# Attention layer with 96 units: projections, output products and row sums gathered in every second unit

## The chip, the core and the metric

The kernel runs on one core of a Trainium2 chip. The time is the device time of one launch in microseconds (us), the median of three runs. Beside these runs there is one execution recorded by the hardware profiler. Its engines are called PE (matrix products), PEld (loading of weights for PE), DVE, ACT and POOL (GpSimd) in the views, and SP issues most of the DMAs.

## What is computed

Four layers work on x of shape (4, 256, 48, 48) in float32: four samples of 2304 positions with 256 channels. Each layer adds its result to x, after a group norm of x. Only the first layer is touched by the change:

```python
def _L0_conv_ref(x, w_qkv, w_out, b_out):        # HEADS = 8, DIM_HEAD = 64, SCALE = 10
    qkv = jnp.einsum('oc,bchw->bohw', w_qkv, x)
    q, k, v = jnp.split(qkv, 3, axis=1)
    q, k, v = map(to_heads, (q, k, v))           # (b, 8, 64, 2304)
    q, k = _l2norm_last(q), _l2norm_last(k)      # over the 2304 positions
    sim = jnp.einsum('bhdi,bhdj->bhij', q, k) * SCALE
    attn = jax.nn.softmax(sim, axis=-1)
    out = jnp.einsum('bhij,bhdj->bhid', attn, v)
    ...
    return jnp.einsum('oc,bchw->bohw', w_out, out) + b_out[None, :, None, None]
...
x = x + _L0_conv_ref(_gn(x), L0_conv_w_qkv, L0_conv_w_out, L0_conv_b_out)
```

Layer 1 is a gate made of a pooled and blurred map with 81 distinct taps a channel; layer 2 is an attention with one head; layer 3 a depthwise convolution with a norm.

## The kernel before

**Phases, units, ticks.** Layer 0 has 16 phases, one for each sample `b` and pair of heads `p`. A phase has `NCH` = 6 units, each a slice of `SL` = 384 query positions (`l0_unit`), so there are 96 units. A unit has `NG` = 9 ticks, each for two blocks of 128 key positions. All units of layers 0 and 2 run in one list, in `attend`. The order of the instructions on every engine is written out by hand: the loop of `attend` issues them tick by tick, and engines run that order, waiting only for each other's results and buffers.

In a tick `attend` issues, in this order:

- `scores` for two key blocks: eight products with 64x64 pieces of the array (the profile records each float32 product twice), then two exponentials on ACT into `pt` tiles (eight buffers, so four ticks' worth). The scores go to `sc` tiles, of which there are two, of two banks each.
- `add_up` for the tick before: two DVE additions of `pt` tiles into `acc`, the row sums. In the first sample every second tick (`PAIRED`) adds its two `pt` tiles on POOL first (`half`, L355).
- what is entered for this tick in `due` and in `fills`, the latter in the order of a rank, and the generators of other layers (`lanes`): layer 1 of sample b-1 runs beside layer 0 of sample b.
- `weigh` for the tick before: eight products `av<-pt,v` with 64x64 pieces.
- `take_taps`: some of the tap products of layer 1 (`tap`, L992, on ACT) that wait in `taps_due`, as many as `QUOTA` says for the slot of the tick in its unit; one more is taken behind each job whose rank is in `EVICTED`.

**The stretch of full-array products.** In the third tick of a unit (slot 2, `AT_CHUNK`), three kinds of job are entered in `fills`:

- `chunk(s)`: the projections of one slice of 384 positions for the next phase: `query` and `key` (`qk`, L661, two float32 products of 128x128 by 384 columns each) and `values` (L695, six of 128 columns). They go to `pj` tiles, of which there are two, and ACT moves them out (L681, L700) and squares q and k (L686). `fetch` loads the x slices, two in advance.
- `total`: the sums over partitions of `acc` of the unit that ended two ticks before (L386, eight products with 128x32 pieces, 96 columns); ACT copies them to `row` and a DMA to `l`. Three ticks later `invert` takes reciprocals on DVE and SP's DMAs spread them to `rinv`; four ticks after that `divide` (POOL, L424) multiplies the output, which `fold` (POOL, L420) has formed.
- `out_proj`: 11 ticks after a unit's end, its two output products (`part`, L759) and their additions onto x on DVE (`onto`, L775). From the second sample on `part(0)` uses an `sc` tile, `part(1)` a `pj` tile.

So each unit of layer 0 has one such stretch between its scores and its `weigh`. The matrix products of the group norms (`of_means`, `of_squares`) and `biased` are put into these stretches too. The strips of layer 1 (`strips`) start when the norm's `nb` is there, and reduce a round of taps on DVE (L1015) in slots 2, 4, 6 and 8; a reduction first issues those of its taps that have not been issued yet.

Of the kernel before, what the change touches and what calls it, by code (L numbers as in the profile page):

```python
# [9 lines left out]
F32 = mybir.dt.float32  # L10
# [4 lines left out]
P = 128  # L15
# [63 lines left out]
def usual_path(  # L79
# [109 lines left out]
    of_k, of_out, clock = {}, {}, {"t": -1}  # L189
# [12 lines left out]
    def gn(b, res, halves=range(NK), slices=range(NSL), first=False, placed=False):  # L202
# [62 lines left out]
        if placed:  # L265

            t = clock["t"] + 1
            t += (AT_AFTER - t) % NG
            fills.setdefault(t, []).extend([(3.1, of_means), (3.3, squares)])
            fills.setdefault(t + NG, []).extend([(3.1, of_squares), (3.3, inverse)])  # L270
            due.setdefault(t + NG + 3, []).append(done)
            yield 1
            return
# [34 lines left out]
    op = main.enter_context(tc.tile_pool(name="o", bufs=2))  # L308
    ppool = main.enter_context(tc.tile_pool(name="pt", bufs=8))
    apool = main.enter_context(tc.tile_pool(name="acc", bufs=2))  # L310
    hpool = main.enter_context(tc.tile_pool(name="half", bufs=3))
# [37 lines left out]
    def add_up(u, g):  # L349
# [3 lines left out]
        if g in u["paired"]:  # L353
            half = hpool.tile([P, 2, SL], F32, tag="half", name="half")
            nc.gpsimd.tensor_add(half, pts[0], pts[1])  # L355
            pts = [half]
            ready, u["terms"] = terms, pts
        else:
            ready, u["terms"] = terms + pts, []
# [17 lines left out]
    def total(u):  # L377

        if of_out.get("t") == clock["t"]:
            ps = of_out["ps"][:, 392 : 392 + QC]  # L380
        else:
            ps = pj_tile()[:, :QC]
        for e in range(2):
            for j in range(4):
# [4 lines left out]
                )  # L389
        row = small.tile([P, QC], F32, tag="row", name="row")  # L390
        nc.scalar.copy(row, ps)  # L391
# [3 lines left out]
    def invert(u):  # L395
        ls = small.tile([P, LW], F32, tag="ls", name="ls")
        nc.vector.reciprocal(ls, u["l"])
        u["rinv"] = rpool.tile([P, SL], F32, tag="rinv", name="rinv")
# [29 lines left out]
    def total_here(u):  # L428
# [4 lines left out]
        u["rinv"] = rpool.tile([P, SL], F32, tag="rinv", name="rinv")  # L433
# [5 lines left out]
    def total_final(u):  # L439
# [12 lines left out]
        u["part"] = rpool.tile([P, SL], F32, tag="rinv", name="rinv")[:, :QC]  # L452
# [34 lines left out]
    EVICTED = (1, 2, 3.2, 4.3)  # L487
    AT_TOTAL, AT_FOLD, AT_INVERT, AT_DIVIDE, AT_AFTER = 3, 2, 5, 9, 11
    AT_CHUNK = AT_AFTER % NG

    def last(u, t):
# [17 lines left out]
        else:  # L509
            at_total = AT_TOTAL if "shift" in u["of"] else AT_CHUNK  # L510
            todo = [
                (fills, at_total, (4.1, lambda: total(u))), (due, AT_FOLD, lambda: fold(u, nc.gpsimd)),
                (due, AT_INVERT, lambda: invert(u)),
                (due, AT_DIVIDE, lambda: divide(u, nc.gpsimd)),
            ]
            after = AT_AFTER
# [77 lines left out]
    def project(b, norm, pair):  # L594
# [109 lines left out]
        def chunk(s):  # L704

            def query():
                qk(s, 0)()
# [2452 lines left out]
```

## Time and profile before

| | |
|---|---|
| median of three runs | 3393.66 us (3392.78 to 3393.75) |
| the profiled execution, its own time | 3394.24 us |
| its span from first to last instruction | 3392.5 us |
| PE, DVE, ACT, POOL busy | 3361.0, 2548.5, 2284.9, 618.3 us |
| granted PE clock | 0.999 |
| first tick of layer 0 to the first of layer 2 (timeline) | 39.98 to 2846.24 us |

The span is what the trace covers; the own time has 1.7 us more around it. Of a group of instructions the views give the line, the engine, the operation, the tiles as out<-in, the shape and the count, then the busy time, the mean of one in ns, and the idle time of the engine just before it with what ended it.

### The profile page before, as it was taken

What the parts mean: (1) busy time and instruction counts of PE and PEld (TensorE: products, weight loads), DVE (VectorE), ACT (ScalarE), POOL (GpSimd) and SP (SyncE); (2) the same over time, 40 slices, a digit from 0 to 9 for tenths busy, and PEclk for the clock granted to TensorE, in tenths of its full rate; (3) what the DMA queues carried; (4) which work ended last, traced back from release to release, by engine and by line L of the source; (5) the groups of instructions that cost most, each with busy time, mean ns of one, the idle gap of its engine ahead of it and who ended that gap; (6) DMA issues with size and microseconds to landing.
All of it is one profiled execution on the core that took longest, in us unless ns stands there. A gap on an engine that the chain in (4) does not pass through costs nothing.

```text
span 3392.5 us, 89388 instructions
## 1 busy us (share of the span) xinstructions
PE 3361.0 (99%) x38014; PEld 1692.1 (50%) x38014; DVE 2548.5 (75%) x3425; ACT 2284.9 (67%) x3680; POOL 618.3 (18%) x617
## 2 busy tenths in 40 slices
PE   9999999999999999999999999999999999999997
PEld 5555555555555555555554555555554444454543
DVE  3456545568788888787988787777887888977877
ACT  5565656555786687556876885658867865555576
POOL 3433333331111001011111000111110110221133
PEclk9999999999999999999999999999999999999999
DMA  2211111111111111131111111111111110231067
GB/s 93 50 24 27 23 27 22 26 22 27 19 32 23 27 16 31 15 87 18 27 23 27 23 27 23 25 23 27 23 23 23 24 26 11 46 73 21 7 161 231
DMA packets 113176, 127.38 MB, mean 38 GB/s; under 512 B 43056, under 2 KB 103424, under 8 KB 112256
## 3 DMA queue, kind: packets, MB, share of 16 engines
q1 hardware_dynamic: 111520, 119.67, 17.5%
q8 instruction: 300, 4.92, 0.6%
q10 hardware_dynamic: 1248, 1.91, 0.2%
q14 instruction: 108, 0.88, 0.1%
HBM read 56.99 MB, written 11.80 MB: 20 GB/s over the span
## 4 chain that ended last, share of the span: by engine, by line
PE 94%; DVE 3%; ACT 1%; issue 0%; DMA 0%; POOL 0%; SPq 0%; DVEq 0%; POOLq 0%; ACTq 0%
PE av L344 37%; PE sc L324 36%; PE pj L661 8%; PE pj L695 4%; PE pj L759 3%; PE pj L386 1%; PE sc L759 1%; DVE acc L373 1%; PE cv L1977 1%; PE pj L1249 1%; PE pj L1102 1%; PE pj L1290 0%; PE pj L1324 0%; DVE sh L1839 0%; DVE pad L1795 0%
## 5 line engine op out<-in xcount | busy, mean ns | idle before, releaser
L330 ACT ACTIVATE pt<-sc 128x768 f32<-128x768 f32 x1944 | 1473.4, 810 | 739.4 <-PE sc L324 727.3
L373 DVE TENSOR_TENSOR acc<-acc,pt 128x768 f32<-128x768 f32 x1534 | 1529.1, 997 | 179.8 <-ACT pt L330 77.0
L344 PE MATMUL av<-pt,v 64*64 64x384 f32 x13824 | 1274.8, 484 | 0.0
L324 PE MATMUL sc<-q,k 64*64 64x384 f32 x13824 | 1270.0, 482 | 0.5 <-ACT pt L330 0.5
L324 PEld LDWEIGHTS sc<-q,k 64*64 64x64 f32 x13824 | 525.4, 133 | 589.5 <-issue 555.1
L344 PEld LDWEIGHTS av<-pt,v 64*64 64x64 f32 x13824 | 518.2, 133 | 568.4 <-issue 521.5
L424 POOL TENSOR_TENSOR o<-o,rinv 128x384 f32<-128x384 f32 x95 | 121.9, 1283 | 1694.6 <-DMA rinv<-rinv 1684.5
L992 ACT ACTIVATE prod<-pd,wt 128x256 f32<-128x256 f32 x486 | 340.6, 761 | 0.2
L775 DVE SCALAR_TENSOR_TENSOR x<-pj,bo,x 128x384 f32<-128x384 f32 x122 | 75.4, 618 | 278.3 <-ACT row L391 207.0
L661 PE MATMUL pj<-xs,w 128*128 128x384 f32 (+1 forms) x720 | 268.9, 496 | 0.0
L355 POOL TENSOR_TENSOR half<-pt 128x768 f32<-128x768 f32 x96 | 176.0, 1833 | 377.5 <-ACT pt L330 316.1
L373 DVE TENSOR_TENSOR acc<-acc,half 128x768 f32<-128x768 f32 x96 | 91.8, 956 | 120.4 <-POOL half L355 120.2
L661 PEld LDWEIGHTS pj<-xs,w 128*128 128x128 f32 x720 | 124.5, 190 | 93.6 <-issue 32.9
L1015 DVE TENSOR_REDUCE prod<-prod 128x256 f32<-128x1280 f32 x114 | 168.8, 1480 | 1.0 <-ACT prod L992 1.0
L344 PE MATMUL av<-pt,qv 64*64 64x384 f32 x1728 | 163.8, 487 | 0.0
L324 PE MATMUL sc<-qv,kd 64*64 64x384 f32 x1728 | 161.9, 482 | 0.0
L695 PEld LDWEIGHTS pj<-w,xs 128*128 128x128 f32 x1080 | 134.5, 191 | 24.1 <-issue 1.2
L367 DVE TENSOR_TENSOR acc<-pt 128x768 f32<-128x768 f32 x108 | 126.2, 1169 | 25.8 <-ACT pt L330 25.6
L695 PE MATMUL pj<-w,xs 128*128 128x128 f32 x1080 | 135.0, 275 | 0.0
L420 POOL TENSOR_TENSOR o<-raw 128x384 f32<-128x384 f32 x95 | 120.3, 1267 | 45.2 <-ACT raw L416 44.2
L416 ACT COPY raw<-av 128x768 f32<-128x768 f32 x108 | 86.4, 800 | 51.1 <-PE av L344 50.1
L700 ACT COPY v<-pj 128x384 f32<-128x384 f32 x96 | 46.0, 479 | 92.3 <-PE pj L695 92.3
(318 smaller groups left out, 2293.6 us busy)
## 6 DMA issues: line engine op xcount, KB each, us to landing
xs<-in_x_dram SPq DMA_DIRECT2D x90, 384.0 KB
sh<-pad SPq DMA_DIRECT2D x122, 162.2 KB
rinv<-rinv SPq DMA_DIRECT2D x208, 94.5 KB
out_dram<-x SPq DMA_DIRECT2D x23, 384.0 KB
w<-in_wqkv_dram SPq DMA_DIRECT2D x32, 192.0 KB
x<-in_x_dram SPq DMA_DIRECT2D x4, 1152.0 KB
x<-in_x_dram SPq DMA_DIRECT2D x9, 384.0 KB
rinv<-ls SPq DMA_DIRECT2D x208, 1.5 KB
```

The costliest lines, as they stand in the source:

```text
L324: nc.tensor.matmul(ps[c * D : (c + 1) * D, h, :SL], lhsT=u["of"]["k"][r, j0 : j0 + D], rhs=u["of"]["q"][r, u["qc"]], start=True, stop=True,)
L330: nc.scalar.activation(pt, ps[:, :, :SL], AF.Exp, scale=u["scale"])
L344: nc.tensor.matmul(u["av"][h * D : (h + 1) * D, half, :SL], lhsT=value(u, j, h)[r], rhs=pt[r, h, :], start=j == 0, stop=j == JB - 1,)
L355: nc.gpsimd.tensor_add(half, pts[0], pts[1])
L367: nc.vector.tensor_add(u["acc"], ready[0], ready[1])
L373: nc.vector.tensor_add(u["acc"], u["acc"], term)
L424: eng.tensor_mul(o, o, u["rinv"])
L661: nc.tensor.matmul(ps[:, :n], lhsT=at["w"][:, k, t, :], rhs=xs[s][:, k, :n], start=k == 0, stop=k == NK - 1,)
L695: nc.tensor.matmul(ps[:, i * P : (i + 1) * P], lhsT=xs[s][:, k, i * P : (i + 1) * P], rhs=at["w"][:, k, 2, :], start=k == 0, stop=k == NK - 1,
L759: nc.tensor.matmul(ps[:, :n], lhsT=wo[:, p, k * P : (k + 1) * P], rhs=o["o"][:, :n], start=True, stop=True,)
L992: nc.scalar.activation(bufs[n % 3][:, :, min(n, 1) + i].rearrange("p (r c) -> p r c", c=AS), pd[:, PAD + dr : PAD + dr + AS, PAD + dc : PA ...
L1015: nc.vector.tensor_reduce(to, bufs[n % 3][:, :, : min(n, 1) + len(taps)], AX.X, ALU.add)
```

## The change

Up to tick `ALONE` (810, the start of the last of the 16 phases), the jobs of the stretch are gathered in the odd units. `place_at` moves a tick that falls into an even unit on by one unit; the first unit of samples 1, 2 and 3 is excepted. Two slices are projected in the odd unit, with ranks 1 to 1.5 for the first and 2 to 4.3 for the second. The totals of two units go to one `pj` tile, and their copies on ACT become a job of their own (`read_total`). The two output products of a unit go to the two banks of one `sc` tile, and its two additions onto x follow together (`both`); two units take both `sc` tiles. `invert`, `divide` and the output products of a unit come up to two units later than before, and `o`, `acc` and `rinv` get one more buffer each. The group norms that run `placed` are moved by the same rule. `fold` comes one tick later. `PAIRED` is dropped: all additions into `acc` are DVE's. From tick 810 on the stretches stay as they were.

```diff
@@ -186,7 +186,7 @@
 
 
     GN_TICKS = NSL + 4
-    of_k, of_out, clock = {}, {}, {"t": -1}
+    of_k, of_out, of_sums, clock = {}, {}, {}, {"t": -1}
 
     WARM = 160
 
@@ -266,9 +266,11 @@
 
             t = clock["t"] + 1
             t += (AT_AFTER - t) % NG
+            t = t if placed == "soon" else place_at(t)
             fills.setdefault(t, []).extend([(3.1, of_means), (3.3, squares)])
-            fills.setdefault(t + NG, []).extend([(3.1, of_squares), (3.3, inverse)])
-            due.setdefault(t + NG + 3, []).append(done)
+            t = place_at(t + NG)
+            fills.setdefault(t, []).extend([(3.1, of_squares), (3.3, inverse)])
+            due.setdefault(t + 3, []).append(done)
             yield 1
             return
         yield 3
@@ -305,10 +307,9 @@
     xsp = keep.enter_context(tc.tile_pool(name="xs", bufs=2))
     big = main.enter_context(tc.tile_pool(name="big", bufs=2))
     wqp = main.enter_context(tc.tile_pool(name="wq", bufs=2))
-    op = main.enter_context(tc.tile_pool(name="o", bufs=2))
+    op = main.enter_context(tc.tile_pool(name="o", bufs=3))
     ppool = main.enter_context(tc.tile_pool(name="pt", bufs=8))
-    apool = main.enter_context(tc.tile_pool(name="acc", bufs=2))
-    hpool = main.enter_context(tc.tile_pool(name="half", bufs=3))
+    apool = main.enter_context(tc.tile_pool(name="acc", bufs=3))
     rpool = main.enter_context(tc.tile_pool(name="rinv", bufs=1))
     lp = main.enter_context(tc.tile_pool(name="l1", bufs=1))
 
@@ -350,13 +351,7 @@
 
         pts = [u["pt"][j] for j in range(g * G, (g + 1) * G)]
         terms = u.setdefault("terms", [])
-        if g in u["paired"]:
-            half = hpool.tile([P, 2, SL], F32, tag="half", name="half")
-            nc.gpsimd.tensor_add(half, pts[0], pts[1])
-            pts = [half]
-            ready, u["terms"] = terms, pts
-        else:
-            ready, u["terms"] = terms + pts, []
+        ready, u["terms"] = terms + pts, []
         if g == NG - 1:
             ready, u["terms"] = ready + u["terms"], []
             if u.get("final"):
@@ -378,8 +373,12 @@
 
         if of_out.get("t") == clock["t"]:
             ps = of_out["ps"][:, 392 : 392 + QC]
+        elif of_sums.get("t") == clock["t"]:
+            ps = of_sums["ps"][:, 128 : 128 + QC]
         else:
-            ps = pj_tile()[:, :QC]
+            of_sums["ps"], of_sums["t"] = pj_tile(), clock["t"]
+            ps = of_sums["ps"][:, :QC]
+        u["sums"] = ps
         for e in range(2):
             for j in range(4):
                 h, q = j // 2, 2 * (j % 2) + e
@@ -387,15 +386,17 @@
                     ps[32 * j : 32 * j + 32], lhsT=step1[:, 16 - 16 * e : 48 - 16 * e],
                     rhs=u["acc"][:, h, q * QC : (q + 1) * QC], start=e == 0, stop=e == 1,
                 )
+
+    def read_total(u):
         row = small.tile([P, QC], F32, tag="row", name="row")
-        nc.scalar.copy(row, ps)
+        nc.scalar.copy(row, u["sums"])
         u["l"] = small.tile([P, LW], F32, tag="l", name="l")
         nc.sync.dma_start(u["l"], row[0 : P : 16, :].rearrange("g (p w) -> g p w", w=LW))
 
     def invert(u):
         ls = small.tile([P, LW], F32, tag="ls", name="ls")
         nc.vector.reciprocal(ls, u["l"])
-        u["rinv"] = rpool.tile([P, SL], F32, tag="rinv", name="rinv")
+        u["rinv"] = rpool.tile([P, SL], F32, tag="rinv", name="rinv", bufs=2)
         for c in HALVES:
             r0 = c.start
             nc.sync.dma_start(
@@ -430,7 +431,7 @@
         ps = pj_tile()
         for h, c in enumerate(HALVES):
             nc.tensor.matmul(ps[c, :SL], lhsT=ones, rhs=u["acc"][:, h, :], start=True, stop=True)
-        u["rinv"] = rpool.tile([P, SL], F32, tag="rinv", name="rinv")
+        u["rinv"] = rpool.tile([P, SL], F32, tag="rinv", name="rinv", bufs=2)
         nc.vector.reciprocal(u["rinv"], ps[:, :SL])
         u["l"] = ps[:, :SL]
         if "shift" not in u["of"]:
@@ -449,7 +450,7 @@
                         rhs=term[:, h, q * QC : (q + 1) * QC], start=i == 0 and e == 0,
                         stop=i == len(terms) - 1 and e == 1,
                     )
-        u["part"] = rpool.tile([P, SL], F32, tag="rinv", name="rinv")[:, :QC]
+        u["part"] = rpool.tile([P, SL], F32, tag="rinv", name="rinv", bufs=2)[:, :QC]
         nc.vector.reciprocal(u["part"], ps)
         u["l"] = ps
 
@@ -484,9 +485,17 @@
         del taps_due[:n]
 
     FREE = 10**6
-    EVICTED = (1, 2, 3.2, 4.3)
+    EVICTED = (1, 1.2, 1.45, 1.5, 2, 2.2, 3.2, 4.3)
     AT_TOTAL, AT_FOLD, AT_INVERT, AT_DIVIDE, AT_AFTER = 3, 2, 5, 9, 11
     AT_CHUNK = AT_AFTER % NG
+    PHASE = NCH * NG
+    ALONE = (B * NPAIR - 1) * PHASE
+
+    def place_at(t):
+
+        while t < ALONE and (t // NG) % 2 == 0 and (t % (NPAIR * PHASE) >= NG or t < NG):
+            t += NG
+        return t
 
     def last(u, t):
 
@@ -507,14 +516,20 @@
                     todo.append((due, 2, lambda: note(u)))
             after = 3
         else:
-            at_total = AT_TOTAL if "shift" in u["of"] else AT_CHUNK
+            two = "shift" in u["of"]
+            at_total = AT_TOTAL if two else place_at(t + AT_CHUNK) - t
+            late = 0 if two else at_total - AT_CHUNK
             todo = [
-                (fills, at_total, (4.1, lambda: total(u))), (due, AT_FOLD, lambda: fold(u, nc.gpsimd)),
-                (due, AT_INVERT, lambda: invert(u)),
-                (due, AT_DIVIDE, lambda: divide(u, nc.gpsimd)),
+                (fills, at_total, (4.1, lambda: total(u))),
+                (fills, at_total, (4.15, lambda: read_total(u))),
+                (due, AT_FOLD + (not two), lambda: fold(u, nc.gpsimd)),
+                (due, AT_INVERT + late, lambda: invert(u)),
+                (due, AT_DIVIDE + late, lambda: divide(u, nc.gpsimd)),
             ]
-            after = AT_AFTER
-        todo += [(fills, after, fn) for fn in u["after"]]
+            after = AT_AFTER + late
+            if not two:
+                after = place_at(t + after) - t
+        todo += [(fills, after, fn) for fn in u["after"](t + after)]
         for when, dt, fn in todo:
             when.setdefault(t + dt, []).append(fn)
 
@@ -703,6 +718,8 @@
 
         def chunk(s):
 
+            early = s % 2 == 0
+
             def query():
                 qk(s, 0)()
 
@@ -715,8 +732,9 @@
                     fetch(s + 2)
 
             return [
-                (1, query), (2, lambda: values(s)), (2.2, lambda: square(s, 0)), (3, key),
-                (3.2, lambda: at["evict"]()), (4.3, end),
+                (1 if early else 2, query), (1.2 if early else 2.2, lambda: values(s)),
+                (1.25 if early else 2.25, lambda: square(s, 0)), (1.4 if early else 3, key),
+                (1.45 if early else 3.2, lambda: at["evict"]()), (1.5 if early else 4.3, end),
             ]
 
         def scale():
@@ -745,15 +763,22 @@
             ],
         }
 
+    outs = {}
+
     def out_proj(b, p, c, pair, o):
 
         cols = slice(c * SL, (c + 1) * SL)
 
         of = {}
+        alone = False
 
         def part(k):
-            of[k] = ps = pj_tile() if k or b == 0 or soon else sc_tile()[:, 0, :]
-            if k:
+            if alone:
+                of[k] = ps = pj_tile() if k or soon else sc_tile()[:, 0, :]
+            else:
+                of["two"] = of["two"] if k else sc_tile()
+                of[k] = ps = of["two"][:, k, :]
+            if k and alone:
                 of_out["ps"], of_out["t"] = ps, clock["t"]
             n = SL + (c == 0)
             nc.tensor.matmul(
@@ -780,13 +805,27 @@
             part(0)
             onto(0)
 
+        def both():
+            onto(0)
+            onto(1)
+
         end = b == B - 1 and p == NPAIR - 1
         soon = end and c >= NCH - 2
-        return [
-            (0.5 if soon else 1.5 if b else 0, first),
-            *[(0.6 if end and c == NCH - 1 else r, fn)
-              for r, fn in ((4, lambda: part(1)), (4.2, lambda: onto(1)))],
-        ]
+
+        def jobs(t):
+            nonlocal alone
+            alone = t >= ALONE
+            if alone:
+                return [
+                    (0.5 if soon else 1.5, first),
+                    *[(0.6 if end and c == NCH - 1 else r, fn)
+                      for r, fn in ((4, lambda: part(1)), (4.2, lambda: onto(1)))],
+                ]
+            n = outs.get(t, 0)
+            outs[t] = n + 1
+            return [(n + 1.1, lambda: part(0)), (n + 1.3, lambda: part(1)), (n + 1.35, both)]
+
+        return jobs
 
     def l0_unit(b, p, c, pair):
         hold = {}
@@ -799,7 +838,7 @@
             return hold["o"][:, :SL]
 
         return {
-            "pt": {}, "qc": slice(c * SL, (c + 1) * SL), "paired": () if b else PAIRED,
+            "pt": {}, "qc": slice(c * SL, (c + 1) * SL),
             "soon": b == B - 1 and p == NPAIR - 1 and c == NCH - 1,
             "scale": 1.0, "of": pair, "o": o_tile,
             "after": out_proj(b, p, c, pair, hold),
@@ -1360,8 +1399,8 @@
 
     def l2_unit(b, c, s2):
         return {
-            "pt": {}, "qc": slice(c * SL, (c + 1) * SL), "of": s2, "after": [],
-            "paired": (), "scale": D ** -0.5,
+            "pt": {}, "qc": slice(c * SL, (c + 1) * SL), "of": s2, "after": lambda t: [],
+            "scale": D ** -0.5,
             "soon": b == B - 1, "final": b == B - 1 and c == L2C - 1,
             "o": lambda: y_of(b)[:, c * SL : (c + 1) * SL],
         }
@@ -1413,7 +1452,7 @@
         norm, norm2 = norms1[b], norms2[b]
         norm2["st"] = small.tile([P, NK, NSL, 6], F32, tag="gn_st2", name="gn_st2")
         start = clock["t"]
-        ahead = gn(b, norm, placed=True)
+        ahead = gn(b, norm, placed="soon")
         for _ in range(NSL - 1):
             yield next(ahead)
         res = {}
@@ -1540,7 +1579,7 @@
             new = projs[i + 1]
             work[0] = [new["start"]]
             for s in range(NCH):
-                work[NG * s + AT_CHUNK] = new["chunk"](s)
+                work.setdefault(NG * (s | 1) + AT_CHUNK, []).extend(new["chunk"](s))
             for slot, fn in zip((n - 5, n - 3, n - 2, n - 1), new["scale"]):
                 work[slot] = [fn]
             if i + 2 < len(order):
```

## Prediction

> **What bounds the kernel now.** I read the page first, then the waits of PE, then a table of windows over single ticks, then the timeline of PE through one stretch, last those of ACT, DVE and POOL.
>
> ```profile
> span 3392.5 us, 89388 instructions
> ...
> PE 3361.0 (99%) x38014; PEld 1692.1 (50%) x38014; DVE 2548.5 (75%) x3425; ACT 2284.9 (67%) x3680; POOL 618.3 (18%) x617
> ...
> PE 94%; DVE 3%; ACT 1%; issue 0%; DMA 0%; POOL 0%; SPq 0%; DVEq 0%; POOLq 0%; ACTq 0%
> ```
>
> PE is busy for 99% and makes 94% of the chain that ended last. The waits of PE between 40 and 2850 us sum to 0.8 us. So layer 0 (2806 us) is as long as PE's own work; only something that makes PE's work shorter, or a new wait of PE, moves the time. But busy is not peak, so the ticks are looked at singly (columns: window, length, busy of PE, PEld, DVE, ACT, POOL with counts, granted clock, DMA):
>
> ```profile
> 1507.52:1510.10 2.58, 2.58 (x36) 1.21 (x32) 2.48 (x3) 2.22 (x3) 2.40 (x2) 1.00 0.11 34
> 1510.10:1518.72 8.62, 8.62 (x76) 4.98 (x72) 5.80 (x11) 4.42 (x10) 0.27 (x1) 1.00 0.01 2
> 44.69:51.55 6.86, 6.86 (x56) 3.90 (x52) 2.87 (x3) 4.41 (x10) 3.73 (x4) 1.00 0.04 4
> ```
>
> A plain tick is 2.58 us, a tick with the full stretch 8.62, one with a slice's projections alone 6.86 (6.87 by the starts). Both lengths repeat through all units within 0.02 us; where a norm's products or `biased` are added it is 8.84 or 9.06. The stretch as PE starts it:
>
> ```profile
> 1510.10 1.47 PE L324 MATMUL sc<-q,k 64*64 64x384 f32 x16
> 1511.50 1.56 PE L661 MATMUL pj<-xs,w 128*128 128x384 f32 x4
> 1512.90 0.81 PE L759 MATMUL sc<-o,wo 128*128 128x385 f32 x2
> 1513.54 1.50 PE L695 MATMUL pj<-w,xs 128*128 128x128 f32 x12
> 1514.88 1.46 PE L661 MATMUL pj<-xs,w 128*128 128x384 f32 x4
> 1516.17 0.81 PE L759 MATMUL pj<-o,wo 128*128 128x385 f32 x2
> 1516.91 0.54 PE L386 MATMUL pj<-acc,step 128*32 128x96 f32 x16
> 1517.38 1.52 PE L344 MATMUL av<-pt,v 64*64 64x384 f32 x16
> 1518.72 1.47 PE L324 MATMUL sc<-q,k 64*64 64x384 f32 x16
> ```
>
> Read start to start, since ends are modelled. A plain tick is 32 records on quarters of the array, eight times 384 columns of the whole array: 0.3225 us for 384 columns. The stretch has 17 times that (projections 12, outputs 4, sums 1): 5.48 us. It takes 8.62 - 2.58 = 6.04, so 0.56 are lost at its joints: scores to projections 0.11 late and 0.11 in the first projection, 0.05 at values to key, 0.10 at outputs to sums, 0.15 in the sums, 0.05 in `weigh`.
>
> **The change part by part.**
>
> *Fewer joints.* Of the 0.56, only the 0.05 inside the projections recurs for the second slice of a gathered stretch: 0.51 are saved for each stretch that vanishes. The 90 units before tick 810 have 90 stretches; after it there are 45, and three more for the first units of samples 1 to 3, which keep totals and outputs: 42 fewer. 42 x 0.51 = 21.4, less 0.1 because the first unit's stretch lacks totals and outputs. Products neither vanish nor are added. **-21.3 us.**
>
> *PSUM tiles in the gathered stretch.* It uses seven `pj` tiles in turn out of two. I laid it out from the tick's start, with the durations of these rows and ACT's spacings when back to back (exponential 0.70, q or k out 0.47, v out 0.38, square 0.51, tap 0.54 to 0.59), with a tap behind each of the first four evictions. The second slice's q is out at 9.44; its key product, which needs that tile, comes at 10.62. Its v is out at 10.56; the sums need that tile at 11.9. ACT ends at about 14.5 at the latest, the next exponential can start at 14.95. The narrowest cover is thus 0.5 us on ACT and 1.2 on a tile. Cost nothing; without the cover a late eviction is paid in full, 45 times.
>
> *Score tiles.* Both now hold output products. The next scores need them at 14.0 and 14.7; DVE's last pair of additions (2 x 0.62, L775) can start at 10.7 and ends at 12.0 when DVE is not behind. Cover 2.6 us; see the rivals.
>
> *ACT between the stretches.* Layer 1's taps need 16 issues a unit. `QUOTA` gives 12, the stretch 4. An even unit has no stretch now, so reductions in its slots 4, 6 and 8 must issue 2, 1 and 1 taps first, on top of the two of the quota. ACT's timeline in a tick with two taps, and at a unit's end:
>
> ```profile
> 946.32 1.29 ACT L992 ACTIVATE prod<-pd,wt 128x256 f32<-128x256 f32 x2
> 947.50 1.51 ACT L330 ACTIVATE pt<-sc 128x768 f32<-128x768 f32 x2
> 949.50 0.80 ACT L416 COPY raw<-av 128x768 f32<-128x768 f32 x1 [0.48 <-PE av L344]
> 950.19 0.77 ACT L992 ACTIVATE prod<-pd,wt 128x256 f32<-128x256 f32 x1
> 950.75 1.54 ACT L330 ACTIVATE pt<-sc 128x768 f32<-128x768 f32 x2
> ```
>
> Two taps fill a tick (1.40 + 1.18 = 2.58). At 950.75 the exponential starts 1.56 after its tick (949.19), 0.67 later than usual, and the next tick still starts on time, at 951.77. Three taps make 0.59 late: free. Four make 1.18: the first exponential is read out at 2.8, when PE wants the tile at 2.58: 0.35 us. That happens in some ten even units (two in each of five of the six runs of taps; the last run lies past tick 810). **+3.5 us**; bounds 0 (if PE's slack is larger) and 13 (if the late taps cost 0.8 in each of the 16 even units).
>
> *DVE between the stretches.* DVE falls behind in plain ticks and catches up in the stretch. Worst are layer 1's maxima: in the unit at 1123 us its additions end 4.7 after the start of the long tick, then come two maxima of 1.6, and it is 1.1 into the next tick when done. As an even unit (the norms below shift layer 1 by one unit) this tick is 2.58 long: 4.7 + 3.2 - 2.6 = 5.3, so 4.2 later. At the unit's end the additions ended 6.9 into the tick; this becomes about 10, as the long tick before leaves DVE 1.2 better off. PE allows about 10.1: four ticks' worth of `pt` tiles, so 3 x 2.58 plus 2.4 for the latest start of an exponential. POOL then decides:
>
> ```profile
> 1507.69 1.00 POOL L424 TENSOR_TENSOR o<-o,rinv 128x384 f32<-128x384 f32 x1 [24.51 <-DMA rinv<-rinv]
> 1507.80 3.39 DVE L373 TENSOR_TENSOR acc<-acc,pt 128x768 f32<-128x768 f32 x2
> 1508.70 1.67 POOL L420 TENSOR_TENSOR o<-raw 128x384 f32<-128x384 f32 x1
> ```
>
> Two additions take 3.39 beside a divide and a fold, against 1.95 alone: 1.44 for 2.67 us of POOL. An even unit has two divides one behind the other, so about 0.7 more. [...] By the row, 1 us of excess in each of three units (the second set of maxima of each sample): **+3 us**[...].
>
> *POOL's additions.* 96 of 1.83 us go (L355), and DVE gets 96 more of 0.96: 92 us over 24 units, 3.8 each, where DVE has at most 21.1 us of 29.7. Hidden by PE: nothing. DVE's 120.2 us of waiting for `half` go too, behind the same cover. If DVE were full there, 92 us would come to light; it has 4.8 left in the worst unit.
>
> *Later totals, divides, outputs.* Two totals' eight `rinv` DMAs are issued together, and POOL waits for them with the next folds behind it. In the trace the divide comes some 10 us after its `invert`; output products now follow after at least 15 ticks. Nothing. On SP the third slice's fetch waits for the key product of the first, with both `l` DMAs behind it, whose rows come later still: nothing.
>
> *Norms.* A squares product that falls into an even unit comes one unit later; layer 1 starts one unit later and has just room to end in its phases. For the third sample one pair falls alone into layer 2: 0.2 (8.84 - 8.62) and a joint of 0.5: **+0.7 us**.
>
> Sum: -21.3 + 3.5 + 3 + 0.7 = -14.1. The profiled execution took 3394.24 (span 3392.5 and 1.7 around it), so 3380.1; the median of the runs is 0.6 lower: 3379.5.
>
> **The rivals.**
>
> *All covers hold* (0.2): no wait of PE, 3394.24 - 20.6 - 0.6 = 3373. For it: PE's total wait of 0.8 us in layer 0 now. Against: no tick with four taps exists in the trace.
>
> *ACT and DVE bind in every even unit with layer 1 work* (0.2): ACT 13 and DVE 7.5 by the upper ends, -21.3 + 13 + 7.5 + 0.7 = -0.1, so 3393.5; halfway from the forecast, 3386.5. Against: a lateness of 0.67 was free.
>
> *Score tiles, the slower side* (0.06): PE waits at the first scores after a gathered stretch until DVE has added both outputs onto x. It decides once DVE reaches these additions over 2.6 us late; to be 0.2% slower, PE must lose 21 + 7 us over 45 stretches, 0.62 in each, so DVE must be 3.2 late in every one. For it: DVE is up to 7 us behind at unit ends. Against: in the long tick DVE waited for PE before L775 (1.03 us in the unit above, 207 us in all), so it had caught up. It would give 3400.
>
> *The stretch isn't gathered as said*, if `pj` or `sc` waits split it, the joints staying (0.06): no change, 3392 to 3394.
>
> **How the numbers follow.** Forecast 0.48, 3375 to 3384; the rivals 0.2, 0.2, 0.06, 0.06. The range 3370 to 3388 takes in the forecast, the first rival (with 3 us for joints that I undercount) and over half of the second. Under 0.2%, 6.8 us, a measurement of this kernel can hardly tell from no change. Faster than 3386.9: 0.48 + 0.2 + 0.12 = 0.8; within, 0.08 of the second rival and 0.06: 0.14; slower 0.06.
>
> **What would show it.** Odd units' long ticks of 14.1 us (2.58 + 11.5) and plain slots 2 in even units; waits of PE for ACT `pt` in slot 5 of even units with taps; of ACT for DVE `acc` at the ends of units with maxima. Waits of PE at `sc` for DVE x would show the slower rival; long ticks over 14.5 would refute the joints.

## The result, and the profile after

| | before | after |
|---|---|---|
| median, range of 18 runs each | 3393.64 us (3392.25 to 3394.57) | 3385.95 us (3383.70 to 3389.17) |
| ratio after to before, 95% interval | | 0.9979 [0.9972, 0.9986] |
| the profiled execution: own time, span | 3394.24, 3392.5 us | 3386.97, 3385.2 us |
| granted PE clock | 0.999 | 0.998 |
| start of tick 865, near the end of layer 0 | 2848.82 us | 2840.68 us |

The change saves 7.7 us of the 14.1 that were forecast. The busy times of the page after:

```profile
PE 3342.8 (99%) x38014; PEld 1703.0 (50%) x38014; DVE 2603.2 (77%) x3521; ACT 2274.3 (67%) x3680; POOL 439.4 (13%) x521
```

PE does the same 38014 instructions in 18.2 us less (3361.0 before), so the joints went. But the span fell by 7.3 only: PE is idle for some 11 us more. In the chain of work that ended last, DMA and POOL, 0% before, now hold 2% and 1%. The waits of PE between 40 and 2840 us (what waits, for whom, total us, times, longest) were 0.8 us in all before:

```profile
PE pj L1312 <- DMA xs<-x_out: 4.5, 1, 4.5
PE sc L784 <- POOL o L425: 4.4, 3, 1.7
PE sc L784 <- ACT pt L331: 1.1, 3, 0.4
PE pj L784 <- ACT qv L1298: 0.6, 1, 0.6
PE sc L325 <- ACT pt L331: 0.5, 1, 0.5
```

But for the last, they fall in four of the 864 ticks of layer 0. Single ticks after, from the windows (columns as in the prediction): a gathered one, the two with four and one tap, the first of sample 1, and tick 812, the first with a stretch in the last phase.

```profile
939.00:953.17 14.17, 14.17 (x117) 8.85 (x117) 7.46 (x11) 10.70 (x26) 1.14 (x2) 1.00 0.10 29
981.54:984.27 2.73, 2.73 (x36) 1.07 (x29) 2.63 (x3) 2.73 (x6) 0.34 (x1) 1.00 0.42 109
984.27:986.94 2.67, 2.67 (x36) 1.18 (x36) 2.64 (x4) 2.67 (x5) 0.00 (x0) 1.00 0.29 86
738.20:746.33 8.13, 6.29 (x60) 2.80 (x56) 4.95 (x10) 1.75 (x3) 2.09 (x3) 1.00 0.45 112
2670.01:2685.24 15.23, 10.06 (x88) 5.42 (x84) 4.30 (x7) 5.72 (x11) 1.94 (x2) 0.89 0.34 84
```

In the first three PE is busy for the whole window. In the fourth it idles for 1.8 us; in the last for 5.2, and the granted clock is 0.89. The gathered tick as PE starts it:

```profile
939.00 1.47 PE L325 MATMUL sc<-q,k 64*64 64x384 f32 x16
940.40 1.56 PE L676 MATMUL pj<-xs,w 128*128 128x385 f32 x4
941.80 0.81 PE L784 MATMUL sc<-o,wo 128*128 128x384 f32 x2
942.44 1.50 PE L710 MATMUL pj<-w,xs 128*128 128x128 f32 x12
943.78 0.81 PE L784 MATMUL sc<-o,wo 128*128 128x384 f32 x2
944.43 2.75 PE L676 MATMUL pj<-xs,w 128*128 128x385 f32 x8
...
949.64 1.45 PE L676 MATMUL pj<-xs,w 128*128 128x384 f32 x4
951.03 0.87 PE L385 MATMUL pj<-acc,step 128*32 128x96 f32 x32
951.82 1.52 PE L345 MATMUL av<-pt,v 64*64 64x384 f32 x16
```

No brackets: no start in the stretch waits for another engine. It takes 14.17 - 2.58 = 11.59 us beyond a plain tick where the forecast said 11.5. Both units' sums stand together (x32), so the passages between shapes of the array (64x64, 128x128, 128x32 and back) occur once.

**Where the time went**, as sums of tick lengths, layer 0, after against before. The row of the joints leaves out the waits of the rows below it: it compares the stretches before tick 810 with those of the run "The small DMAs of both units ahead of the four broadcasts" (next section), in which these waits are gone.

| part of the prediction | forecast | measured |
|---|---|---|
| joints | -21.3 | -22.0 |
| four taps in a tick | +3.5 | +2.45 |
| DVE's lateness | +3 | 0 |
| "Later totals, divides, outputs": first units of samples 1 to 3 | 0 | +5.2 |
| same, x fetch of the last phase: tick 812 | 0 | +7.1 |
| norm products that left tick 857 for layer 2 (-0.64), and the start (-0.22) | 0 | -0.9 |
| sum, to tick 865 | -14.8 | -8.1 |

Past tick 865 come +0.8 us, of them 0.5 for the norm products that now stand alone in a tick of layer 2 (forecast 0.7).

One more new wait is hidden in the row of the joints: `PE sc L784 <- ACT pt L331`, 1.1 us in three. In the first units of samples 1 to 3 no projection stands between the scores and the output products any more, so PE waits 0.38 us in each until ACT has read the `sc` tile.

**The two large missed waits have one cause, on SP's queue.** At the first unit of sample 1 (SP's timeline: start, us to issue, operation):

```profile
724.07 1.16 SPq L402 DMA_DIRECT2D rinv<-ls  x2
725.84 1.61 SPq L407 DMA_DIRECT2D rinv<-rinv  x2
727.62 4.54 SPq L402 DMA_DIRECT2D rinv<-ls  x2
734.01 1.62 SPq L407 DMA_DIRECT2D rinv<-rinv  x2
```

```profile
734.26 1.01 POOL L425 TENSOR_TENSOR o<-o,rinv 128x384 f32<-128x384 f32 x1 [11.89 <-DMA rinv<-rinv]
741.99 0.99 POOL L425 TENSOR_TENSOR o<-o,rinv 128x384 f32<-128x384 f32 x1 [6.72 <-DMA rinv<-rinv]
```

```profile
743.04 1.56 PE L784 MATMUL sc<-o,wo 128*128 128x384 f32 x4 [1.46 <-POOL o L425]
```

Each unit issues two small DMAs (`rinv<-ls`, 1.5 KB) and then two broadcasts (`rinv<-rinv`, 94.5 KB each). Two units are now inverted together, so the second unit's small DMAs stand behind the first one's broadcasts: they take 4.54 us to issue where the first took 1.16, and 6.37 to land where the first took 1.75. The second divide comes 7.7 us after the first, and PE waits. Larger DMAs show the same: two fetches of 384 KB took 4.26 us to issue right behind two broadcasts before the change (below), and the later ones of layer 2, with no broadcast right ahead, 0.53 to 0.59 each (four in either trace).

It shows in few places. Where two units inverted together also have their output products together, these come at least 15 ticks after the `invert`, but for four ticks: 218, 434 and 650, the first units of samples 1 to 3, which are excepted from the gathering, and 812. There they come after 6, as all did before the change.

At tick 812 the fetch of x for layer 2 stands behind such a pair of units, too. Before the change it was issued 9.4 us ahead of the tick (which started at 2685.91), behind one unit's DMAs:

```profile
2674.89 1.58 SPq L406 DMA_DIRECT2D rinv<-rinv  x2
2676.52 4.26 SPq L1243 DMA_DIRECT2D xs<-x_out  x2
```

After it, 2.6 us ahead of the tick's start at 2670.01:

```profile
2659.37 4.55 SPq L402 DMA_DIRECT2D rinv<-ls  x2
2665.72 1.63 SPq L407 DMA_DIRECT2D rinv<-rinv  x2
2667.40 4.64 SPq L1282 DMA_DIRECT2D xs<-x_out  x2
```

```profile
2676.02 1.39 PE L1312 MATMUL pj<-w,xs 128*64 128x64 f32 x24 [4.54 <-DMA xs<-x_out]
2677.34 2.69 PE L784 MATMUL sc<-o,wo 128*128 128x384 f32 x4
```

The four records of L784 take 2.69 us here, 1.53 to 1.56 elsewhere. The windows by the microsecond show why (granted clock third from the end):

```profile
2676.00:2677.00 1.00, 0.98 (x22) 1.00 (x24) 0.00 (x0) 0.00 (x0) 0.00 (x0) 0.62 0.02 8
2677.00:2678.00 1.00, 1.00 (x9) 0.73 (x7) 0.00 (x0) 0.55 (x2) 0.00 (x0) 0.50 0.00 0
2678.00:2679.00 1.00, 1.00 (x3) 0.55 (x2) 0.00 (x0) 1.00 (x3) 0.00 (x0) 0.50 0.00 0
2679.00:2680.00 1.00, 1.00 (x3) 0.56 (x3) 0.62 (x1) 0.44 (x1) 0.00 (x0) 0.67 0.00 0
```

After the idle stretch PE runs at half clock, for 3.41 us up to 2679.66: 0.38 + 0.5 + 0.5 + 0.33 = 1.7 us lost. Tick 812 was 6.83 before; the two output products of one more unit make 1.29 (counted under joints), and 4.54 + 0.62 (for `qv`) + 1.7 leave 0.25 of the 15.23 without a row.

### The profile page after: what moved, and what is told of

Its sections match the earlier page's. It is cut to its first block, busy times and chain, and to the rows that moved or that the text cites. A ratio compares the mean times of both kernels' runs of the same rounds, so it can differ in the third digit from the quotient of the medians.

```text
span 3385.2 us, 89674 instructions
## 1 busy us (share of the span) xinstructions
PE 3342.8 (99%) x38014; PEld 1703.0 (50%) x38014; DVE 2603.2 (77%) x3521; ACT 2274.3 (67%) x3680; POOL 439.4 (13%) x521
## 4 chain that ended last, share of the span: by engine, by line
PE 92%; DVE 3%; DMA 2%; ACT 1%; issue 1%; POOL 1%; SPq 1%; DVEq 0%; POOLq 0%; ACTq 0%
PE av L345 35%; PE sc L325 35%; PE pj L676 8%; PE pj L710 4%; PE sc L784 3%; DVE acc L368 1%; PE pj L385 1%; PE cv L2016 1%; PE pj L1288 1%; DMA rinv<-ls 1%; PE pj L1141 1%; DMA rinv<-rinv 1%; PE pj L1329 0%; PE pj L1363 0%; DVE sh L1878 0%
## 5 line engine op out<-in xcount | busy, mean ns | idle before, releaser
L331 ACT ACTIVATE pt<-sc 128x768 f32<-128x768 f32 x1944 | 1475.9, 812 | 720.6 <-PE sc L325 704.3
L368 DVE TENSOR_TENSOR acc<-acc,pt 128x768 f32<-128x768 f32 x1726 | 1710.2, 991 | 300.1 <-ACT pt L331 189.5
L1031 ACT ACTIVATE prod<-pd,wt 128x256 f32<-128x256 f32 x486 | 328.2, 758 | 0.3
L800 DVE SCALAR_TENSOR_TENSOR x<-sc,bo,x 128x384 f32<-128x384 f32 x181 | 105.1, 614 | 229.2 <-PE sc L784 228.1
L676 PE MATMUL pj<-xs,w 128*128 128x384 f32 (+1 forms) x720 | 259.2, 492 | 0.0
L676 PEld LDWEIGHTS pj<-xs,w 128*128 128x128 f32 x720 | 132.3, 190 | 108.3 <-issue 22.1
L784 PE MATMUL sc<-o,wo 128*128 128x384 f32 (+1 forms) x362 | 147.6, 493 | 5.5 <-POOL o L425 4.4
L362 DVE TENSOR_TENSOR acc<-pt 128x768 f32<-128x768 f32 x108 | 111.5, 1032 | 51.0 <-ACT pt L331 51.0
L325 PEld LDWEIGHTS sc<-qv,kd 64*64 64x64 f32 x1728 | 68.9, 133 | 70.9 <-issue 69.7
## 6 DMA issues: line engine op xcount, KB each, us to landing
rinv<-rinv SPq DMA_DIRECT2D x208, 94.5 KB
```

The source lines that it names most:

```text
L325: nc.tensor.matmul(ps[c * D : (c + 1) * D, h, :SL], lhsT=u["of"]["k"][r, j0 : j0 + D], rhs=u["of"]["q"][r, u["qc"]], start=True, stop=True,)
L331: nc.scalar.activation(pt, ps[:, :, :SL], AF.Exp, scale=u["scale"])
L362: nc.vector.tensor_add(u["acc"], ready[0], ready[1])
L368: nc.vector.tensor_add(u["acc"], u["acc"], term)
L676: nc.tensor.matmul(ps[:, :n], lhsT=at["w"][:, k, t, :], rhs=xs[s][:, k, :n], start=k == 0, stop=k == NK - 1,)
L784: nc.tensor.matmul(ps[:, :n], lhsT=wo[:, p, k * P : (k + 1) * P], rhs=o["o"][:, :n], start=True, stop=True,)
```

## The experiments

The theory: joints and taps are what the prediction said, and the missing time is those two waits, with one cause. The first rival: a wait that is mended only uncovers that of the next engine, and little comes back. The second: gathering the projections alone has the gain, and where the sums stand doesn't matter. The kernel before ran beside each of three groups: medians 3393.32 us (up to the four taps), 3393.35 (projections only, sums apart, POOL's additions, six tiles) and 3392.94 (projections only with the sums first, and the last kernel).

**The changed kernel once more**, as the measure of the group.

> The changed kernel itself, on the chip of the next three runs. Expected 3386 us, within 2. All theories: gathered ticks of 14.16 us, waits of PE for the divide (POOL) at the first unit of samples 1 to 3 and for the x_out fetch at the start of the last phase of layer 0.

Measured: 3387.67 (3385.02 to 3391.55), ratio 0.9984 [0.9976, 0.9991]. The ticks 218, 434, 650 and 812 took 8.11, 8.54, 8.04 and 16.03 us. Its runs spread over 6.5 us, those of before over 2.8. The same waits stand in this trace, and tick 812 differs from the first profile's by 0.8 (its half clock lasted until 2681).

**The small DMAs of both units ahead of the four broadcasts** (in the runs below: the rows first).

```diff
+    def spread_rows(u):          # the two broadcasts of invert
-                (due, AT_INVERT + late, lambda: invert(u)),
+                (due, AT_INVERT + late, (5, lambda: invert(u))),
+                (due, AT_INVERT + late, (5.5, lambda: spread_rows(u))),
```

> The small DMAs of both units' inverted sums are issued ahead of the four broadcasts. Theory (the second divide is late because SP holds its small DMAs behind the first unit's broadcasts): its small DMAs go out some 3.5 us earlier, the output products of the three first units of samples 1 to 3 no longer wait 1.5 us for POOL, and with their joints the three ticks fall from 8.0-8.5 to 6.4 or less: 4 to 5 us in all, 3381. Rival (the broadcasts themselves fill the DMA engines): both divides come late, nothing gained, 3386, or worse where the first divide was in time.

Measured: 3375.05 (3373.01 to 3376.14), ratio 0.9946 [0.9932, 0.9960]: 12.6 less than the changed kernel in the same group, more than expected. SP's and POOL's timelines at the same place:

```profile
724.00 2.43 SPq L402 DMA_DIRECT2D rinv<-ls  x4
726.48 6.46 SPq L411 DMA_DIRECT2D rinv<-rinv  x4
```

```profile
734.95 1.00 POOL L427 TENSOR_TENSOR o<-o,rinv 128x384 f32<-128x384 f32 x1 [12.66 <-DMA rinv<-rinv]
738.27 1.00 POOL L427 TENSOR_TENSOR o<-o,rinv 128x384 f32<-128x384 f32 x1 [2.31 <-issue]
```

The small DMAs issue at once and the second divide comes 3.3 us after the first, not 7.7. The first units' ticks are 6.40, 6.52 and 6.52, so 5.25 less in sum. The rest is that I had not seen that the order of the small DMAs also moves the fetch, which stands behind all eight: it is now issued at 2659.99 for a tick at 2664.75, its wait is gone, and with it the half clock: tick 812 takes 9.18 and not 16.03. 5.25 + 6.85 = 12.1. (Between the two profiled executions layers 2 and 3 also differ by 3.5 us, which the edit doesn't touch.)

**The fetch of x for layer 2 seven ticks earlier (in tick 804, not 811).**

```diff
-                fetch(0)
-                fetch(1)
+            phases[-1][1].setdefault(n - 6, []).append(start.ahead)   # does both
```

> The two x_out fetches of layer 2's first projection are issued five ticks earlier, ahead of the inverted sums' DMAs. Theory (the fetch stands behind two units' DMAs on SP instead of one's): the 4.5 us wait of PE at the start of the last phase goes and the tick of 15.2 us falls to 8.2 to 10, so 5 to 7 us less, 3380. Rival (the tick is long because its output products wait for the divide as well): only 1 to 3 us go, 3384; the DMAs of the sums are now behind the fetch.

Measured: 3384.32 (3382.52 to 3387.05), ratio 0.9974 [0.9963, 0.9986]: 3.4 less than the changed kernel, so where the rival put it. Tick 812 takes 10.82 in the profiled execution (16.03 in that of the changed kernel of this group); why the median gained less was not followed. The wait for DMA is gone and the clock stays at 1.00, but a wait for POOL that had been hidden behind it shows (PE's timeline in the tick):

```profile
2674.97 0.91 PE L784 MATMUL sc<-o,wo 128*128 128x384 f32 x2 [1.54 <-POOL o L425]
```

So this half of the rival holds: mending one consumer uncovers the next, as long as the second unit's `rinv` is late. Both consumers were freed by the order of the small DMAs alone, in the run before this one.

**Four taps in the bare slot 2 of even units**, to keep the reductions of slots 4, 6 and 8 from issuing any late.

```diff
-            take_taps(QUOTA[clock["slot"]])
+            bare = t < ALONE and clock["slot"] == AT_CHUNK and (t // NG) % 2 == 0
+            take_taps(4 if bare else QUOTA[clock["slot"]])
```

> In the bare slot 2 of an even unit four taps are taken. Theory (PE waits behind ticks with four taps): no reduction has to issue taps first, the ticks of 2.73 and 2.67 us behind them are 2.58 again, ten times 0.24, so 2.4 us less, 3383.5. Rival (those ticks are long for another reason, for instance DVE): they stay, 3386.

Measured: 3392.51 (3390.86 to 3394.69), ratio 0.9998 [0.9989, 1.0006]: 4.8 more than the changed kernel, against what I expected. My arithmetic was wrong: four taps overfill the tick in slot 2 as well. In the 16 even units with taps slots 3 and 4 now take 2.77 to 2.87 and 2.68 us. Slots 5 and 6 are plain again in all of them, as the theory said, but the plain ticks' excess over 2.58 rises from 2.63 to 5.59. That is 3.0 of the 4.8; the rest was not followed. The run shows the price of four taps, not a cure for it.

**Only the projections gathered**; sums, output products and norms stay in every unit.

```diff
     def place_at(t):
-        while t < ALONE and (t // NG) % 2 == 0 and (t % (NPAIR * PHASE) >= NG or t < NG):
-            t += NG
         return t
```

> Only the projections of two slices are gathered; totals, output products and norms stay in every unit as before the change (one sc tile, ranks as in the changed kernel). Theory (a joint between 64x64 and full-array products costs 0.5 us, and the gain is the number of such joints): there are as many joints as before the change, so its time, 3393, plus 2.4 for the ticks with four taps: 3394 to 3396. Rival (the gain comes from running the projections of two slices together): 3381 to 3385.

Measured: 3416.87 (3415.65 to 3417.22), ratio 1.0069 [1.0055, 1.0083], far above what both expected. A wait of PE makes 17.5 of the 23.5 us over the kernel before:

```profile
PE sc L782 <- ACT pt L331: 17.5, 43, 0.5
```

In an even unit the output products now follow right behind the scores, and need the `sc` tile that ACT still reads for its exponentials: 0.41 us, 43 times. It is the wait that the changed kernel has three times. Even ticks take 5.11. The experiment measured another wait than it was made for.

**The same, with the sums ahead of the output products in even units**, so that ACT is done with the tile.

```diff
-                (fills, at_total, (4.1, lambda: total(u))),
+                (fills, at_total,
+                 (1.05 if not two and t + at_total < ALONE and (t + at_total) // NG % 2 == 0 else 4.1,
+                  lambda: total(u))),
```

> Only the projections gathered, as in the earlier run of that kind, but in even units the sums come ahead of the output products, so that these don't meet an sc tile that ACT still reads. Theory (joints alone, and in the earlier run a wait of 0.41 us in 43 even units): that wait goes, and the time is that of before the change plus the ticks with four taps, 3394 to 3398. Rival (gathering the projections by themselves costs or gains): below 3390 or above 3402.

Measured: 3399.02 (3396.90 to 3400.44), ratio 1.0018 [1.0011, 1.0026]. That wait is gone. An even and an odd tick with their stretches:

```profile
1157.77:1162.47 4.70, 4.70 (x56) 2.13 (x52) 3.34 (x6) 1.64 (x3) 1.10 (x2) 1.00 0.03 4
1124.59:1137.13 12.54, 12.54 (x96) 7.83 (x92) 11.90 (x15) 7.32 (x19) 1.24 (x2) 1.00 0.12 33
```

Even ticks take 4.70, so 2.12 for five times 384 columns (1.61): 0.51 lost. Odd ones take 12.55: 9.97 for 29 times (9.35): 0.62 lost. Together 1.13, twice the 0.56 of before: gathering the projections alone saves no joint. The second rival falls. The kernel is 6.1 us slower than before, above what was expected; its trace has 2.3 of that in long ticks and 3.5 in plain ones, of which 1.0 in two ticks where the next scores wait for DVE's additions onto x, the wait of the slower rival in the prediction.

**The sums of the second unit apart**, between the second slice's products.

```diff
-                (fills, at_total, (4.1, lambda: total(u))),
+                (fills, at_total, (2.4 if late else 4.1, lambda: total(u, late > 0))),   # own pj tile
```

> The changed kernel with one of the two units' sums moved ahead of the second slice's key product, into a pj tile of its own: 41 stretches get one more passage from full-array products to 128x32 pieces and back. Theory (a passage costs by itself): 0.10 + 0.15 and about as much back, 0.3 to 0.4 in each, 12 to 16 us more than the changed kernel: 3400 to 3404. Rival (the loss at the joints is in the scores' or values' hand-over, not in the change of the pieces): under 3 us more, 3388 to 3391.

Measured: 3403.17 (3400.48 to 3407.07), ratio 1.0030 [1.0019, 1.0041]: 15.5 more than the changed kernel, as expected, for no added product. PE's timeline at the end of a stretch:

```profile
658.99 0.54 PE L387 MATMUL pj<-acc,step 128*32 128x96 f32 x16
659.45 1.56 PE L678 MATMUL pj<-xs,w 128*128 128x384 f32 x4
660.94 0.54 PE L387 MATMUL pj<-acc,step 128*32 128x96 f32 x16
```

No brackets, so no wait. The gathered tick takes 14.50 and not 14.17: one more passage to 128x32 pieces and back costs 0.33 us (0.5 in four ticks), 14.4 in the 41. Joints are a cost of the order of the products; what in a passage takes the time, the change of the pieces or the loading of the next weights, no run separates.

**POOL's additions to DVE, alone**, in the kernel before.

```diff
-PAIRED = (1, 3, 5, 7)
+PAIRED = ()
```

> The kernel before with the additions on GpSimd alone taken away (PAIRED empty). Theory (PE hides both): the time of before, 3393.3, within 1; DVE busy 90 more, POOL 176 less. Rival (POOL and DVE delay each other and through the sums PE): more than 2 us either way.

Measured: 3392.56 (3391.63 to 3393.15), ratio 0.9997 [0.9989, 1.0006]. The page has DVE at 2604.7 and POOL at 428.7 us (2548.5 and 618.3 before), and tick 865 starts at 2848.61 (2848.82): this part of the change is worth nothing, as forecast. The busy times were not: DVE has 56 us more and POOL 190 less, where 90 and 176 were expected.

**Six `pt` tiles and not eight**, to see how much of DVE's lateness the tiles cover.

```diff
-    ppool = main.enter_context(tc.tile_pool(name="pt", bufs=8))
+    ppool = main.enter_context(tc.tile_pool(name="pt", bufs=6))
```

> The changed kernel with six pt tiles in place of eight. Theory (DVE's lateness in even units with maxima, up to 9.2 us in the trace, is covered by four ticks' worth of pt tiles, about 10.1 us): with three ticks' worth, 7.5 us, PE waits where DVE is later than that, 0.7 and 1.7 us in two pairs of units of each sample, 5 to 8 us in all: 3393 to 3396. Rival (the pt tiles don't bind, DVE has other slack): as the changed kernel, 3387.

Measured: 3393.69 (3391.86 to 3395.55), ratio 1.0002 [0.9993, 1.0011]: 6.0 more than the changed kernel, as expected. Plain ticks lose 8.77 and not 2.63, and this line of the waits grows from 0.5 (once, with eight):

```profile
PE sc L325 <- ACT pt L331: 3.3, 10, 0.6
```

**The rows first, and two taps in the bare slot 2**: the version that the runs pointed to.

```diff
-            take_taps(QUOTA[clock["slot"]])
+            bare = t < ALONE and clock["slot"] == AT_CHUNK and (t // NG) % 2 == 0
+            take_taps(2 if bare else QUOTA[clock["slot"]])
```

(and the edit of the rows as above)

> The small DMAs of both units ahead of the broadcasts, as in the run with the rows first, and two taps (not four) in the bare slot 2 of an even unit. Theory (a tick holds two taps beside its exponentials, and PE waits only behind four): no tick gets four taps, 2.4 us less than with the rows first alone: 3372 to 3373.5. Rival (the waits only move on to ticks with three taps): as with the rows first, 3375.

Measured: 3373.03 (3372.00 to 3378.27), ratio 0.9941 [0.9928, 0.9955]: the fastest of all. The plain ticks' excess falls to 0.19 us, that of before, so all of the cost of four taps in a tick is gone. By their times alone this version and the rows without it (0.9946) are not told apart. Its profiled execution happened to be the 3378.27: there the fetch came 2.3 us late to tick 812, and PE fell to half clock again.

```profile
2666.06 0.92 PE L1316 MATMUL pj<-w,xs 128*64 128x64 f32 x24 [2.31 <-DMA xs<-x_out]
2666.91 2.54 PE L788 MATMUL sc<-o,wo 128*128 128x384 f32 x4
```

```profile
2666.00:2667.00 1.00, 0.94 (x25) 0.90 (x25) 0.00 (x0) 0.00 (x0) 0.00 (x0) 1.00 0.03 9
2667.50:2668.00 0.50, 0.50 (x3) 0.20 (x2) 0.00 (x0) 0.50 (x2) 0.00 (x0) 0.50 0.00 0
```

The tick took 13.09 us there against 9.18 in the profiled execution with the rows first, which had no wait for the fetch. The fetch was issued 4.5 us ahead of the tick here and 4.8 there, so it is still near its limit. The rows first and an earlier fetch together were not tried.

## Why the prediction was right, and where it was not

The time lies in the range, and the gain has the cause that was forecast. One term of nothing was wrong by 12.3 us, and costs that came out smaller than forecast made up for part of it.

- *Fewer joints* (-21.3): right. The stretches up to tick 810 hold 550.2 us beyond plain ticks before, and 526.9 in the kernel with the rows first, where the waits are gone; 1.29 of that are two output products that moved past 810, so -22.0. 14.17 us for the tick with 14.1 forecast; with the second unit's sums apart 14.4 us (ticks) or 15.5 (medians) come back; with the projections alone gathered nothing is saved. The rest between -21.3 and -22.0 has two parts: norm products and `biased` next to the sums cost 0.11 and 0.33 where they cost 0.22 and 0.44, 1.8 less in all, and the three waits for ACT in the excepted units cost 1.1.
- *PSUM tiles, score tiles* (0): right for the gathered stretches. None of their starts waits, so both covers held, and the rivals that needed them to fail fall. In the three excepted units the output products wait 1.1 us for ACT at the score tile; the prediction did not look there.
- *ACT between the stretches* (+3.5): mechanism and place right, size not. Ten pairs of ticks as in the second and third window above, at slots 5 and 6 of even units; 0.15 + 0.09 = 0.24 each where 0.35 was the term. Two taps moved to slot 2 took all of it away.
- *DVE between the stretches* (+3): the way was right, the sizes were not, and the term came to 0. DVE reaches 9.2 us behind (unit 38, slot 6) against an allowance of 10.1, and PE never waits for it. Some 1.7 of the 9.2 are POOL's: L972 and L973 take 2.28 and 0.99 us beside a divide and a fold, where the same two operations took 1.42 and 0.18 in the unit at 1123 us before. So the interference came, and was larger than the 1 us that I added; it was the count of about 10 without it that was too high. The six tiles show that the allowance covers the lateness: one tick less of it cost 6.0.

```profile
1153.27 2.28 DVE L972 TENSOR_TENSOR t<-t 128x1222 f32<-128x1222 f32 x1
1155.47 0.99 DVE L973 COPY t<-t 128x26 f32<-128x26 f32 x1
```

```profile
1153.25 1.01 POOL L425 TENSOR_TENSOR o<-o,rinv 128x384 f32<-128x384 f32 x1 [7.06 <-DMA rinv<-rinv]
1154.22 2.20 POOL L421 TENSOR_TENSOR o<-raw 128x384 f32<-128x384 f32 x1
```

- *How DVE and POOL disturb each other* (the 7.5 in the second rival): this was the author's estimate of an upper end, with all of POOL's 2.67 us at 1507 us, and 1.0 of a second divide, charged to DVE. No trace shows that much. In the rows above the divide starts 0.02 us ahead of L972, which ends 1.29 us after it (the same operation took 1.42 before, at 1136.43 us); the fold comes while L972 runs, and ends 0.87 us after that, where a fold takes 1.0 alone. The additions (L368) of the trace after, up to 2840 us, go the same way. Of those beside just one divide or fold, 69 started first and took 0.94 to 0.96 us as they do alone, while the POOL instruction took up to 1.81; 50 started second, and 46 of these ended 0.81 to 0.82 us after POOL's end. In the prediction's rows at 1507 us each addition came second: 0.76 and 0.61 us lost, not 2.67.
- *POOL's additions* (0): right, by the run of this part alone.
- *Later totals, divides, outputs* (0): **the step that failed**, by 12.3 us. Two sentences of it did. "Output products now follow after at least 15 ticks" is true of the gathered units; in the units that the change itself excepts, and in tick 812, they follow after 6. And of SP's queue I followed the fetches inside a phase, not the first fetch of the next layer, and not what two units' `rinv` DMAs do to each other when they are issued together. The trace of before had the numbers to ask: the fetch 9.4 us ahead of its tick, and four DMAs for each unit, of which the second two are broadcasts.
- *Norms* (+0.7): 0.5 in layer 2. But the products that moved there had cost 0.64 in tick 857, which the sum did not take off, so -0.2.

So the forecast's mechanism carried the gain, and 12.3 us of missed waits were partly offset by 3 for DVE, 1.05 for ACT and 0.7 for the joints, and by 0.7 for the norms and what follows layer 0: 5.5 us. That the time lies in the range is in part luck: with these terms as forecast, the same waits would have made it about 3391, past 3388. The time lies past the forecast's own 3384, on the near half of "ACT and DVE bind", but not by that rival's mechanism: ACT cost 2.45 and DVE nothing.

What stays open: why DMAs right behind two broadcasts took SP so long to issue (4.26 to 4.71 us for two) was not tested beyond the order; and part of the spread of layers 2 and 3 between executions (3.5 us between two of them) was not followed.

## What to carry to other kernels

Passages between shapes of the array are a cost to be counted like products: 0.5 us for a stretch that need not exist, 0.33 for one split in two. When jobs of two units are gathered, follow their DMAs along the issuing queue to every consumer, the excepted units and the next layer's first fetch above all, and issue all small DMAs ahead of the large ones that depend on them (12.6 us here). When a slot is emptied, find new places for the small jobs of other engines that it used to take (here ACT's taps), or they pile up in the next slots (2.45 us here). And ask whether the emptied slot kept two instructions apart: without the projections the output products met an `sc` tile that ACT was still reading (0.38 us in each of three ticks).

## What was not expected of the hardware

- Two small DMAs behind two broadcasts of 94.5 KB took 4.54 us to issue on SP; without them ahead, 1.16. Two fetches of 384 KB took 4.26 to 4.64 behind two broadcasts; with none right ahead one took 0.53 to 0.59. With the small DMAs issued first the kernel was 12.6 us faster.
- When an addition of DVE (L368) met one divide or fold of POOL, the loss went with which started first. The 69 that started first took 0.94 to 0.96 us, as alone, and the POOL instruction up to 1.81, where it takes 1.0 alone; of the 50 that started second 46 ended 0.81 to 0.82 us after POOL's end. The smallest lead among the 69 was 0.02 us.
- A wait of PE cost more than itself where the granted clock fell. With the wait of 4.54 us came 3.41 us at half clock (1.7 lost); with one of 4.64, in the changed kernel's second profiled execution, half clock in every microsecond from 2675 to 2681; with one of only 2.31, in the last kernel, 3.4 us of it, and there the clock fell 1.3 us after the work had resumed. With the waits of 1.46 and 1.54 us it stayed at 1.00. What decides whether a wait of some 2 us costs the clock was not shown.
- Being 9.2 us late cost DVE's users nothing with four ticks of buffers, and 6.0 us with three.
